# A graph network's first layernorm in blocks of sixteen tiles, one written order for VectorE and ScalarE, and signs taken of integers

## The chip, the core and the metric

The kernel runs on one core of a Trainium2 chip. The core has TensorE (PE in the profile; its weight loads are PEld), VectorE (DVE), ScalarE (ACT), GpSimd (POOL) and SyncE (SP, which only issues DMAs here). Each engine works through its own queue in order; semaphores tie the queues together. The metric is the device time of one execution in microseconds (us); three runs of the kernel before gave a median of 927.64 us.

## What is computed

Two layers of a graph network over N = 6250 nodes of 64 features and E = 206250 edges, sorted by destination:

```python
edge_index = jnp.stack([src, dst])
h = jnp.maximum(_layernorm(x, axis=-1), 0.0)
x = x + _L0_gnn_ref(h, edge_index, ...)      # twice: agg = segment_sum(h[src], dst); relu((h+agg) @ Wa + ba) @ Wb + bb
h = jnp.maximum(_layernorm(x, axis=-1), 0.0)
x = x + _L1_gnn_ref(h, edge_index, ...)      # segment_sum of an MLP of h[src], then an MLP of [h, sum]
```

`_layernorm` is (x - mean) / sqrt(var + 1e-5) over the 64 features. The three segment sums run over the same edges.

## The kernel before

**The graph as a matrix.** The nodes are cut into NT = 49 tiles of 128. The kernel counts, for each tile of destinations, how often each source occurs, and so builds the adjacency matrix A, 49 tiles of 128 x 6272 bytes. A segment sum is then a product of A with the node values on TensorE. The first sum uses each tile of A while it is in SBUF; all tiles are also written to DRAM, and the second and third sums (the two calls of `sweep`, whose products are on L733) read A back from there.

**Building a tile of A** (`build`, L423 to 439). Edges are handled in batches: batch 0 is one pair of tiles, batches 1 to 12 are two pairs (four tiles) each. For a batch b:

- `search(b)` (L291): ScalarE takes signs of 375 samples of `dst` against a bound (L303), VectorE makes the row and base from the sums (L307, L308).
- `fetch_blocks(b)` (L310): GpSimd issues an indirect DMA per pair that fetches a block of 550 integers of `dst` (L316). There are four buffers for them (`blk`, bufs=4).
- `search_block(b, i)` (L320): ScalarE casts the block in place from int32 to float32 (L326), then takes the Sign of it with a sum (L328).
- `fetch_edges(b)` (L331): VectorE makes offsets (L336, L337), GpSimd issues one indirect DMA per pair for destinations (`d_win`) and one for sources (`s_win`), both on L341.
- `slots(b)` (L347): VectorE splits the edges' numbers into word, byte and high part (L366 to L382); `cast` (L384) and `turn` (L390) bring them into the layout of `lkw` through ScalarE and TensorE.
- `hot` (L402), part of `build`: VectorE makes one-hot tables `there`, `high` and `low` (L409, L413, L416). TensorE multiplies them (`cnt`, L432, 64 products of 49 columns a tile, in four quarters of 16), ScalarE writes the counts out as `a` (L434), SP sends the tile to DRAM (L438). Tile 0 is counted in three pieces of 16, 16 and 32 columns (`FIRST_HOTS`), each with tables of its own.

**The first sum.** While tile t is counted, `FirstSum.quarter` multiplies tile t-1 with the layernormed node values `hp` (L587: 49 products of 193 columns; L589: the node itself), a quarter after each quarter of counts. It needs `hp` of all 49 tiles: quarter i uses its i-th fourth. For each four tiles a small MLP (`first_halves` to `third_product`) follows, placed by the table `beside` at quarters of later tiles.

**The first layernorm** (`values(t)`, L503) fills `hp`, eight tiles (XT) a call: TensorE transposes x (L509), a copy goes to SBUF (L512: VectorE for the first four calls, ScalarE for the last three), TensorE subtracts the mean by a product with `center` (L518) into a PSUM bank, `scaled` (L239) squares on ScalarE (L243), sums on VectorE (L245), takes the root on ScalarE (L246), the reciprocal and the scaled, clipped value on VectorE (L247, L248); `split` (L251) makes three bfloat16 parts, whose sum is the value, by turns on ScalarE (L254, L257) and VectorE (L256, L258). The last call has one tile. The calls stand between the steps of batches 0 to 3: `values(0)` after `fetch_blocks(1)`, two more before `slots(0)`, one after `turn(0, 0)`, three after `build(0)`.

**What sets the order.** A scheduler places the instructions; a written order binds it only where the kernel says so. `behind(op, other)` puts `op` after `other` on the same engine without a semaphore. `follow(op, engine)` does that with the engine's last step of `build` (`counted`), so it has no effect until the first `hot`. `search` and `slots` also have a parameter `after`. GpSimd has only the indirect DMAs to issue, in the order written.

Of the kernel before, what the change touches and what calls it, by code (L numbers as in the profile page):

```python
# [31 lines left out]
FP = mybir.dt.float32  # L32
# [6 lines left out]
AF = mybir.ActivationFunctionType  # L39
OP = mybir.AluOpType  # L40
# [5 lines left out]
D = 64  # L46
# [106 lines left out]
def fast(ctx: ExitStack, tc: tile.TileContext, x, src, dst, w, bad, out):  # L153
# [13 lines left out]
    def bank(name, dtype=FP):  # L167
        return pmix.tile([P, CH * 4 // mybir.dt.size(dtype)], dtype, tag="mix", name=name)
# [43 lines left out]
    ps = bank("ps_smp")  # L212
    nc.tensor.matmul(ps[:, :NB], ones[:SP_ROWS, :], smp_d.rearrange("p a b -> p (a b)"), start=True, stop=True)
    smp = once.tile([P, NB], FP, name="smp")
    nc.scalar.copy(smp, ps[:, :NB])


    HP = NP * D + 1
# [29 lines left out]
        return nc.vector.scalar_tensor_tensor(to, xm, 0.0, var[:, :, None].to_broadcast([P, n, D]), op0=OP.max,  # L248
                                              op1=OP.mult)

    def split(parts, v, n, f):  # L251

        p1, p2, p3 = (parts[:, :, i * f:(i + 1) * f] for i in range(NP))
        nc.scalar.copy(p1, v)  # L254
        r = work.tile([P, CH // f, f], FP, name="r", tag=f"r{f}")[:, :n, :]
        nc.vector.tensor_tensor(r, v, p1, op=OP.subtract)  # L256
        nc.scalar.copy(p2, r)  # L257
        nc.vector.tensor_tensor(p3, r, p2, op=OP.subtract)  # L258

    def halves(parts, v):  # L260

        first = nc.scalar.copy(parts[:, :, 0, :], v)
# [16 lines left out]
    def tiles_of(b):  # L279
        return range(starts[b], starts[b] + BATCHES[b]), slice(starts[b], starts[b] + BATCHES[b])  # L280

    counted = {}

    def behind(op, other):

# [4 lines left out]

    def follow(op, engine):  # L291

        if engine in counted:
            behind(op, counted[engine])

    def search(b, after=None):

        if b >= len(BATCHES):
            return
        each, qs = tiles_of(b)  # L300
        for q in each:
            junk = wins.tile([P, NB], BF, name="junk", bufs=1)
            op = nc.scalar.activation(junk, smp, AF.Sign, bias=below_node[:, q:q + 1], accum_out=sign1[:, q:q + 1])  # L303
            if after:
                behind(op, after)
            follow(op, "ACT")
        nc.vector.tensor_scalar(row[:, qs], sign1[:, qs], -0.5, NB / 2 - 1, op0=OP.mult, op1=OP.add)  # L307
        nc.vector.tensor_scalar(base[:, qs], sign1[:, qs], -0.5 * BLK, (NB / 2 - 1) * BLK + BLK / 2,  # L308
                                op0=OP.mult, op1=OP.add)

# [9 lines left out]
    def search_block(b, i):  # L320

        if b >= len(BATCHES):
            return
        q = starts[b] + i
        blk = blks.pop(q)
        follow(nc.scalar.copy(blk.bitcast(FP), blk), "ACT")  # L326
        junk2 = wins.tile([P, BLK], BF, name="junk2", bufs=1)
        return nc.scalar.activation(junk2, blk.bitcast(FP), AF.Sign, bias=below_node[:, q:q + 1],  # L328
                                    accum_out=sign2[:, q:q + 1])

    def fetch_edges(b):  # L331

        if b >= len(BATCHES):
            return
        each, qs = tiles_of(b)
        nc.vector.scalar_tensor_tensor(off_f[:, qs], sign2[:, qs], -0.5, base[:, qs], op0=OP.mult, op1=OP.add)  # L336
        nc.vector.tensor_scalar(off[:, qs], off_f[:, qs], float(E - P), None, op0=OP.min)  # L337
        lists[b] = [wins.tile([P, MOST, P], I32, name=name)[:, :len(each), :] for name in ("d_win", "s_win")]
        for win, of in zip(lists[b], (dst, src)):
            for i, q in enumerate(each):  # L340
                nc.gpsimd.indirect_dma_start(  # L341
                    out=win[:, i, :], out_offset=None, in_=of.rearrange("(a o) -> a o", o=1),
                    in_offset=bass.IndirectOffsetOnAxis(ap=off[:, q:q + 1], axis=0))

    numbers = {}

    def slots(b, after=None):  # L347

        if b >= len(BATCHES):
            return  # L350
# [8 lines left out]

        def first(op):  # L360
            follow(op, "DVE")
            if after:
                behind(op, after)

        pair = temp("pair")
        first(nc.vector.tensor_scalar(pair, d, 1, PITCH // 2 - 1, op0=OP.logical_shift_right, op1=OP.bitwise_and))  # L366
# [25 lines left out]
    def turn(b, i):  # L392

        if b >= len(BATCHES):
            return
        ps = bank("ps_win", BF)
        for k in range(3):
            follow(nc.tensor.transpose(ps[:, k * P:(k + 1) * P], parts2[b % 2][:, i, k, :], identb), "PE")
        lkw = lkws[starts[b] + i] = wins.tile([P, 3, P], BF, name="lkw", bufs=5)
        return nc.scalar.copy(lkw.rearrange("p a b -> p (a b)"), ps[:, :3 * P])  # L400

    def hot(lkw, g0, n):  # L402

# [96 lines left out]
            nc.tensor.matmul(ps[:, j * HID:(j + 1) * HID], t2[:, j * P:(j + 1) * P], w.w3, start=True, stop=True)  # L500
        halves(h2r[:, t:t + n], ps[:, :n * HID].rearrange("p (t f) -> p t f", f=HID))

    def values(t):  # L503

        n = min(XT, NT - t)
        ps = bank("xt")
        sides = [(j, min(2, n - j) * D) for j in range(0, n, 2)]
        for j, f in sides:
            nc.tensor.transpose(ps[:f, j * D:j * D + P], xs[:, t + j:t + j + f // D, :].rearrange("p t d -> p (t d)"), w.ident)  # L509
        f = sides[-1][1]  # L510
        xt = work.tile([P, CH], FP, name="xt", tag="t1")
        op = (nc.vector.tensor_copy if t < 4 * XT else nc.scalar.copy)(xt[:f, :len(sides) * P], ps[:f, :len(sides) * P])  # L512
        if t < 2 * XT:
            behind(op, sampled)
            behind(op, bounds)
        xm = pacc.tile([P, CH], FP, name="acc")
        for j, f in sides:
            nc.tensor.matmul(xm[:, j * D:j * D + f], xt[:f, j * D:j * D + P], center[:f, :f], start=True, stop=True)  # L518
        h = work.tile([P, XT, D], FP, name="h")[:, :n]
        op = scaled(h, xm[:, :n * D].rearrange("p (t d) -> p t d", d=D), n)  # L520
        split(hp[:, t:t + n], h, n, D)
        return op


    beside = {}
# [22 lines left out]
                beside.setdefault(4 * (4 * g + u) + 1, []).append((what, (of,)))  # L548

    nc.gpsimd.memset(hp[:, :, NP * D:], 1.0)  # L550
    search(0)
    fetch_blocks(0)
    search(1)
    fetch_blocks(1)
    values(0)
    search_block(0, 0)
    fetch_edges(0)
    values(XT)
    op = values(2 * XT)
    slots(0, op)  # L560
    cast(0, 0)
    cast(0, 2)
    for i in range(2):
        search_block(1, i)
    fetch_edges(1)
    op = turn(0, 0)
    values(3 * XT)
    search(2, op)
    fetch_blocks(2)
    search(3, op)  # L570
    fetch_blocks(3)

    r1, acc1 = {}, {}

# [32 lines left out]
    for t in range(NT + 1):  # L607
        last_total, total = total, FirstSum(t - 1, a) if t else None
        if t < NT:
            def between(i):  # L610
                if total:
                    total.quarter(i)
                if last_total and i == 2:
                    last_total.check()
                for what, args in beside.get(4 * t + i, ()):
                    what(*args)

            a = build(t, between)
            if t == 0:
                values(4 * XT)  # L620
                for i in range(2):
                    search_block(2, i)
                fetch_edges(2)
                values(5 * XT)
                values(6 * XT)
            if t == 1:
                w1p = weight_halves(w.w1x, "w1p", once)
                m1p, u1p = weight_halves(w.m1x, "m1p"), weight_halves(w.u1x, "u1p")
        else:
            last_total.check()  # L630
            for i in range(4):
                total.quarter(i)
            total.check()
# [368 lines left out]
```

## Time and profile before

| what | value |
|---|---|
| three runs | 929.69, 927.28, 927.64 us; median 927.64 |
| the profiled execution | 924.73 us, of which the span of its core is 922.9 us |
| busy in the span | PE 867.1 us (94%), DVE 619.3 us (67%), ACT 573.9 us (62%), POOL 114.7 us (12%) |
| first `there` on DVE (tile 0) | 25.02 us |
| first product with `hp` (L587) | 53.75 us |
| last product with `hp` (L589), end of the first sum | 394.68 us |
| first and second sweep (L733) | 396 us to the end |
| the casts of L326 | 25, 644 ns each |

How to read it: times in lines of the timeline are the start in us from the span's beginning, then the duration in us, the engine, the line of the kernel, the operation, output and input with their shapes, and in brackets how long the engine was idle before and who released it. A row of a window gives, after the window, its length, and for each engine its busy time and the number of instructions that begin there, then the TensorE clock that was granted (1.00 is full), the share of the DMA engines and GB/s. The profiled execution took 2.9 us less than the median of the runs; durations come from it, and a change is carried as a difference.

### The profile page before, as it was taken

The numbers are of one execution on the slowest core, as the hardware profiler recorded it, in microseconds if no ns is written. First come the engines' busy times: TensorE is split into PE (matmuls) and PEld (weight loads), VectorE is DVE, ScalarE is ACT, GpSimd is POOL, SyncE is SP. The second block draws the span as 40 slices with busy tenths as digits, with TensorE's granted clock in tenths as the row PEclk, the third lists the DMA queues.
The fourth block names the chain that finished last, engine by engine and source line by source line (L and its number), as shares of the span: only waits on it lengthen the run. The fifth ranks groups of instructions, "written<-read, shape, count | busy, mean of one in ns | idle before, by whom it ended". The sixth has DMA issues, their size and how long they took to land.

```text
span 922.9 us, 19818 instructions
## 1 busy us (share of the span) xinstructions
PE 867.1 (94%) x8323; PEld 743.4 (81%) x8323; DVE 619.3 (67%) x914; ACT 573.9 (62%) x772; POOL 114.7 (12%) x86
## 2 busy tenths in 40 slices
PE   3579999999999999999999999999999999999996
PEld 2479898898988999988787777778889767777785
DVE  5899988898888989644554445545445756666652
ACT  5577786667866666654445454454545677877763
POOL 3356423244232200000000000000000000000000
PEclk8599999999999999999999999999999999999999
DMA  6233433334333332555544444444433768888872
GB/s 145 98 118 143 176 133 129 131 143 172 137 118 142 119 141 107 182 134 141 140 118 121 123 115 117 128 119 128 118 103 94 193 176 231 233 224 221 234 188 64
DMA packets 195655, 133.71 MB, mean 145 GB/s; under 512 B 35204, under 2 KB 186884, under 8 KB 195556
## 3 DMA queue, kind: packets, MB, share of 16 engines
q1 hardware_dynamic: 188728, 121.22, 44.5%
q0 software_dynamic: 3600, 10.32, 3.7%
q8 instruction: 67, 1.10, 0.5%
q10 hardware_dynamic: 3228, 0.81, 0.4%
q14 instruction: 32, 0.26, 0.1%
HBM read 91.38 MB, written 40.94 MB: 143 GB/s over the span
## 4 chain that ended last, share of the span: by engine, by line
PE 83%; ACT 6%; issue 5%; DMA 3%; POOL 1%; DVE 1%; DVEq 0%; ACTq 0%; POOLq 0%
PE acc L733 42%; PE acc L587 20%; PE cnt L432 8%; PE ps_t L461 7%; PE ps_y L470 4%; ACT a L434 2%; DMA a<-A 2%; ACT ar L726 1%; PE ps_g L500 1%; PE tf L445 1%; DVE ar L726 1%; POOL d_win L341 1%; ACT blk L326 1%; POOL blk L316 1%; DMA s_win<-in_src_dram,off 1%
## 5 line engine op out<-in xcount | busy, mean ns | idle before, releaser
L726 DVE CAST ar<-a 128x2048 fp32r<-128x2048 uint8 (+2 forms) x208 | 220.4, 1071 | 202.8 <-PE acc L733 163.7
L726 ACT CAST ar<-a 128x2048 fp32r<-128x2048 uint8 (+2 forms) x130 | 234.3, 1804 | 139.3 <-PE acc L733 104.4
L733 PE MATMUL acc<-ar,h2r 128*128 128x512 f32 (+2 forms) x1274 | 297.4, 388 | 0.0
L733 PEld LDWEIGHTS acc<-ar,h2r 128*128 128x128 f32 x1274 | 229.7, 188 | 50.0 <-issue 5.7
L587 PE MATMUL acc<-hp,a 128*128 128x193 bf16 x2401 | 237.0, 247 | 10.7 <-ACT a L434 4.0
L434 ACT ACTIVATE a<-cnt 128x784 int16<-128x784 f32 x196 | 159.6, 820 | 87.1 <-PE cnt L432 63.8
L587 PEld LDWEIGHTS <-a 128*128 128x128 fp8e4 x2401 | 195.9, 98 | 14.3 <-ACT a L434 6.8
L733 PE MATMUL acc<-ar,yr 128*128 128x512 f32 (+2 forms) x637 | 158.4, 399 | 0.5 <-DVE yr L263 0.5
L733 PEld LDWEIGHTS acc<-ar,yr 128*128 128x128 f32 x637 | 115.5, 188 | 33.1 <-issue 10.3
L432 PE MATMUL cnt<-high,low 128*128 128x49 bf16 x3136 | 117.8, 187 | 14.7 <-DVE low L416 9.0
L432 PEld LDWEIGHTS <-low 128*128 128x128 fp8e4 x3136 | 109.6, 97 | 23.2 <-issue 13.3
L416 DVE TENSOR_TENSOR low<-there,lkw 128x2048 int32<-128x2048 bf16 (+2 forms) x51 | 112.0, 2196 | 0.0
L413 DVE TENSOR_TENSOR high<-high,lkw 128x3136 bf16<-128x3136 bf16 (+2 forms) x51 | 87.8, 1722 | 31.0 <-PE cnt L432 30.4
L316 POOL DMA_INDIRECT blk<-in_dst_dram,row x25 | 54.2, 2167 | 126.3 <-DVE base L308 110.4
L409 DVE TENSOR_TENSOR there<-word,lkw 128x2048 bf16<-128x2048 bf16 (+2 forms) x51 | 58.9, 1173 | 0.0
L341 POOL DMA_INDIRECT d_win<-in_dst_dram,off x25 | 26.3, 1052 | 68.8 <-DVE high_i L373 54.3
L341 POOL DMA_INDIRECT s_win<-in_src_dram,off x25 | 32.0, 1281 | 7.6 <-issue 7.6
L463 ACT ACTIVATE t<-ps_t,d 128x512 f32<-128x512 f32 (+2 forms) x26 | 17.3, 666 | 11.7 <-PE ps_t L461 11.7
L463 ACT ACTIVATE t<-ps_t,c 128x512 f32<-128x512 f32 (+1 forms) x26 | 17.1, 663 | 7.5 <-PE ps_t L461 7.5
L463 ACT ACTIVATE t<-ps_t,e 128x512 f32<-128x512 f32 (+2 forms) x26 | 17.2, 663 | 5.4 <-PE ps_t L461 5.4
L448 ACT ACTIVATE h3f<-tf 128x512 fp32r<-128x512 f32 (+2 forms) x13 | 7.5, 574 | 19.2 <-PE tf L445 19.2
L328 ACT ACTIVATE junk<-blk,below_node 128x550 bf16<-128x550 f32 x25 | 18.8, 753 | 0.6
(135 smaller groups left out, 620.1 us busy)
## 6 DMA issues: line engine op xcount, KB each, us to landing
a<-A SPq DMA_DIRECT2D x264, 256.0 KB
A<-a SPq DMA_DIRECT2D x49, 784.0 KB
a<-A SPq DMA_DIRECT2D x24, 192.0 KB
a<-A SPq DMA_DIRECT2D x24, 128.0 KB
a<-A SPq DMA_DIRECT2D x22, 64.0 KB
out_dram<-o SPq DMA_DIRECT2D x11, 128.0 KB
xs<-in_x_dram ACTq DMA_DIRECT2D x3, 256.0 KB
xs<-in_x_dram SPq DMA_DIRECT2D x3, 256.0 KB
```

The source lines that it names most:

```text
L316: nc.gpsimd.indirect_dma_start(out=blks[q], out_offset=None, in_=dst.rearrange("(r b) -> r b", b=BLK), in_offset=bass.IndirectOffsetOnAxis ...
L341: nc.gpsimd.indirect_dma_start(out=win[:, i, :], out_offset=None, in_=of.rearrange("(a o) -> a o", o=1), in_offset=bass.IndirectOffsetOnAx ...
L409: nc.vector.tensor_tensor(there, word2[:, None, :, :].to_broadcast(shape), of(0)[:, :, None, :].to_broadcast(shape), op=OP.is_equal)
L413: nc.vector.tensor_tensor(high, high2[:, None, :, :].to_broadcast(shape), of(1)[:, :, None, :].to_broadcast(shape), op=OP.is_equal)
L416: counted["DVE"] = nc.vector.tensor_tensor(low.rearrange("p (g i) w -> p g i w", i=2), there.rearrange("p g w i -> p g i w"), of(2)[:, :, ...
L432: counted["PE"] = nc.tensor.matmul(ps[:, b, j * H:(j + 1) * H], low[:, g, :], high[:, g // 2, :, g % 2], start=True, stop=True)
L434: counted["ACT"] = nc.scalar.activation(a[:, :, k:k + 2 * PG].rearrange("p h (b j) -> p h b j", b=2), ps[:, :, :PG * H].rearrange("p b (j ...
L461: nc.tensor.matmul(ps[:, :n * P], wt, rhs, start=(i == 0), stop=(i == len(terms) - 1))
L463: nc.scalar.activation(to, ps[:, :n * P], AF.Relu, bias=bias)
L587: nc.tensor.matmul(acc[:, t % 2, :], self.a[:, k, :], hp[:, k], start=(k == 0), stop=False)
L726: widen(ar.rearrange(f"p k t b -> {order}"), a.rearrange(f"p t (k b) -> {order}", b=P))
L733: nc.tensor.matmul(acc[:, :n * P], part, ar[:, k - k0].rearrange("p t b -> p (t b)"), start=(k == 0 and i == 0), stop=(k == H - 1 and i == ...
```

## The change

- `values` is replaced by a class `Values` with one method a step. Blocks a, b and c have 16 tiles each, d has the 49th. Transposes and copies still go eight tiles at a time (`center`), and all copies are on VectorE now; square, sum, root, scaled value, three parts and two remainders are single instructions over 1024 elements instead of two over 512. The centered values lie in a pair of PSUM banks of the counts' pool (`cnt`), the temporaries in the buffers of `there`, `low` and `high`.
- Until tile 0 is counted, `follow` ties every step of VectorE and ScalarE that it is called for to the step before it on that engine (`starting`), so that their order is the written one. The list at the start is written anew: blocks a, b and c come almost whole before `slots(0)`; the last part of c and most of d come after `build(0)`.
- `search_block` loses its cast: Sign reads the int32 block directly. This holds for all 25 blocks.

GpSimd's order of DMAs is the same in both.

```diff
     def follow(op, engine):
 
-        if engine in counted:
+        if starting is not None:
+            if engine in starting:
+                behind(op, starting[engine])
+            starting[engine] = op
+        elif engine in counted:
             behind(op, counted[engine])
...
-        follow(nc.scalar.copy(blk.bitcast(FP), blk), "ACT")
         junk2 = wins.tile([P, BLK], BF, name="junk2", bufs=1)
-        return nc.scalar.activation(junk2, blk.bitcast(FP), AF.Sign, bias=below_node[:, q:q + 1],
-                                    accum_out=sign2[:, q:q + 1])
+        op = nc.scalar.activation(junk2, blk, AF.Sign, bias=below_node[:, q:q + 1], accum_out=sign2[:, q:q + 1])
+        follow(op, "ACT")
...
-    def values(t):
...
+    class Values:
...
+        def center(self, c):
...
+            follow(nc.vector.tensor_copy(xt[:f, :len(sides) * P], ps[:f, :len(sides) * P]), "DVE")
+            if c == 0:
+                self.xm = (pacc.tile([P, CH], FP, name="acc") if n == 1 else
+                           pcnt.tile([P, 2, CH], FP, name="cnt").rearrange("p b c -> p (b c)"))
...
+        def square(self):
...
+            follow(nc.scalar.activation(self.sq, self.xm, AF.Square), "ACT")
+        def variance(self):
...
+            follow(nc.vector.tensor_reduce(self.var, self.sq, axis=AX.X, op=OP.add), "DVE")
...
+        def third(self):
+            follow(nc.vector.tensor_tensor(self.part(2), self.r, self.part(1), op=OP.subtract), "DVE")
...
     search(0)
     fetch_blocks(0)
+    a.center(0)
+    a.center(1)
     search(1)
     fetch_blocks(1)
-    values(0)
+    b.center(0)
+    a.square()
+    b.center(1)
+    a.variance()
+    a.root()
     search_block(0, 0)
+    b.square()
+    a.scale()
     fetch_edges(0)
-    values(XT)
-    op = values(2 * XT)
-    slots(0, op)
+    c.center(0)
+    b.variance()
+    a.first()
+    c.center(1)
+    b.root()
+    a.rest()
+    b.scale()
+    a.second()
+    c.square()
+    c.variance()
+    b.first()
+    a.third()
+    c.root()
+    b.rest()
+    search_block(1, 0)
+    c.scale()
+    b.second()
+    search_block(1, 1)
+    fetch_edges(1)
+    c.first()
+    b.third()
+    slots(0)
     cast(0, 0)
     cast(0, 2)
-    for i in range(2):
-        search_block(1, i)
-    fetch_edges(1)
-    op = turn(0, 0)
-    values(3 * XT)
-    search(2, op)
+    c.rest()
+    turn(0, 0)
+    c.second()
+    d.center(0)
+    search(2)
     fetch_blocks(2)
-    search(3, op)
+    d.square()
+    d.variance()
+    d.root()
+    d.scale()
+    d.first()
+    search(3)
     fetch_blocks(3)
+    starting = None
...
             if t == 0:
-                values(4 * XT)
+                c.third()
+                d.rest()
+                d.second()
+                d.third()
                 for i in range(2):
                     search_block(2, i)
                 fetch_edges(2)
-                values(5 * XT)
-                values(6 * XT)
```

## The prediction

> **What bounds the kernel now.** I read the page first: PE is busy 94% of the span, and 83% of the chain that ended last is PE's. Then the busy time by stage, since the change only touches the start:
>
> ```profile
> core 0: us, PE busy (x) PEld busy (x) DVE busy (x) ACT busy (x) POOL busy (x), PEclk, DMA share, GB/s
> ...
> 20.00:40.00 20.00, 6.80 (x82) 5.85 (x83) 17.45 (x48) 10.77 (x26) 8.41 (x8) 0.50 0.28 80
> 40.00:60.00 20.00, 14.32 (x164) 12.81 (x163) 17.37 (x38) 17.57 (x42) 10.41 (x8) 0.79 0.35 126
> 60.00:80.00 20.00, 19.55 (x361) 19.25 (x359) 20.00 (x22) 13.58 (x25) 8.71 (x4) 1.00 0.24 94
> 80.00:395.00 315.00, 302.56 (x5263) 290.19 (x5261) 273.33 (x355) 218.62 (x372) 80.08 (x52) 1.00 0.39 144
> ```
>
> PE is short of work until about 60 us and nearly full from there to the end. DVE is the other full engine: 20.00 of 20 us between 60 and 80. So the time after 60 us is fixed work, and the question is when, and with how much done, the kernel gets into it. The chain of waits shows what ends the start: GpSimd's DMAs for blocks and edges from 46 to 57.6 us, then DVE's slots, then PE. The timeline of GpSimd has the links:
>
> ```profile
> 46.03 2.24 POOL L316 DMA_INDIRECT blk<-in_dst_dram,row  x1 [11.34 <-ACT junk L328]
> 48.58 2.03 POOL L316 DMA_INDIRECT blk<-in_dst_dram,row  x1 [0.30 <-issue]
> 50.91 0.94 POOL L341 DMA_INDIRECT d_win<-in_dst_dram,off  x1 [0.30 <-DVE off L337]
> 52.16 1.44 POOL L341 DMA_INDIRECT d_win<-in_dst_dram,off  x1 [0.30 <-issue]
> 53.91 0.94 POOL L341 DMA_INDIRECT s_win<-in_src_dram,off  x1 [0.30 <-issue]
> 55.16 0.94 POOL L341 DMA_INDIRECT s_win<-in_src_dram,off  x1 [0.30 <-issue]
> ```
>
> Two blocks of batch 4 stand ahead of the edges of batch 2, in both kernels. They take 10.07 us, and the edges land 1.5 us after the last. DVE stands with tile 3's tables behind those edges:
>
> ```profile
> 45.67 1.78 DVE L413 TENSOR_TENSOR high<-high,lkw 128x3136 bf16<-128x3136 bf16 x1
> ...
> 47.51 2.28 DVE L416 TENSOR_TENSOR low<-there,lkw 128x2048 int32<-128x2048 bf16 x1
> ...
> 57.72 0.29 DVE L373 TENSOR_SCALAR high_i<-s_win 128x256 int32<-128x256 int32 x1 [0.16 <-DMA s_win<-in_src_dram,off]
> ...
> 60.47 1.78 DVE L413 TENSOR_TENSOR high<-high,lkw 128x3136 bf16<-128x3136 bf16 x1
> ...
> 62.37 2.28 DVE L416 TENSOR_TENSOR low<-there,lkw 128x2048 int32<-128x2048 bf16 x1
> ```
>
> I take the start of tile 3's `low`, 62.37 us, as the mark: before it waits rule, after it DVE and PE run without holes. The change is worth what it does to this mark, to PE's arrears at it, and to the steady stage.
>
> **The change, part by part.**
>
> *Prices.* DVE steps of 512 float32 follow each other at 0.60 us (17.10, 17.70, 18.30); 1024 elements took 1.14 (`low` of 128x1024 at 36.42, next at 37.56). ACT: 0.51 for 512; from 0.60 long at 512 and 0.82 at 784, 1.01 long and 0.91 apart at 1024. So a pair of 512 steps becomes one step cheaper by 0.06 us on DVE (four steps, three blocks: 0.7 us) and 0.1 us on ACT. The size itself saves under 2 us, all in a stretch with holes. The order is what counts. I walked the built program's order with these prices.
>
> *To the first edges.* The row for batch 0 now precedes the first copy: blocks leave 0.25 us earlier. But block a needs two copies (9.34 and 9.94), its mean product runs 10.05 to 12.7 (2.68 us before), b's eight transposes to 13.8, b's copies to 14.5, and a's 1024-sum stands behind these in the written order: 14.5 to 15.6, root 0.30, scaled value 16.2 to 17.3. Batch 0's offsets stand behind it and a copy of c (0.60): ready at 18.1 instead of 15.7. Behind this wait is only GpSimd: `d_win` leaves at 18.2, not 15.98; that is hidden, since slots(0) is later still.
>
> *To slots(0).* Between the offset and slots(0) DVE now has eight 1024 steps (9.1), a copy (0.6) and small ones (0.6), and waits twice for ACT: for the second part of a and the square of c in a row (0.7), and for the sign of block (1, 1) (0.7). 18.1 + 11.7 = 29.8 us. Before, slots(0) began at 20.41. The edges have lain there since about 23.
>
> *To the first count.* slots(0) holds now one remainder (1.14) instead of two 512 steps, and ends in the same 1.2 us of cast, transpose and copy as before: 4.1 us instead of 4.6. First `there` 33.9 (25.02 before), first `low` 34.7 (25.84). PE has nothing to do for these 9 us; that costs nothing by itself, since this layernorm work is then no longer in the way.
>
> *To tile 1.* From the first `low` to the end of tile 1's took 16.8 us before (25.84 to 42.6). Four 512 steps leave it (2.4), one 1024 step and the 49th tile's small ones enter (1.7), the waits stay about equal: 16.1. It ends at 50.8 instead of 42.6. The row of batch 4's search is the next step of DVE, as before.
>
> *To the mark.* Before, GpSimd had to wait at this point for a block buffer until 46.03; now the buffers are free, and it starts at 51.0, 5.0 us later. Are its six DMAs again 10.07 us? Alone such an issue takes 0.94 and 0.30 between: 7.5 for six. The row says why they took more: the one from 46.03 ended at 48.27, 0.90 after DVE's `high` left (47.37); the next at 50.61, 0.90 after `low` left. They now start again beside `there`, `high` and `low`, of tile 2. The Trainium skill (SBUF — State Buffer, section Who interferes with whom) speaks against this change here: GpSimd and VectorE share one pair of ports, VectorE takes it with two SBUF inputs or in a two-port mode, and the second to come is blocked until the first is through. By that rule and the row: 10.1; without it 7.5, and the mark 2.6 us earlier. I take 10.1: edges issued at 61.1, landed at 62.6. From there DVE has high part, word, parts, `high` and two shifts ahead of `low`: 0.20 + 0.20 + 0.33 + 1.70 + 0.40 = 2.8 (4.65 before, with layernorm and weight steps between, which now come earlier). The mark: 65.4, that is 3.0 us later.
>
> *PE's arrears.* Layernorm being done, tiles 0 and 1 get their first-sum products sooner: at the mark about 22 products of 193 columns more are done, at 0.085 us each 1.9 us. If PE alone ruled afterwards, 3.0 - 1.9 = 1.1 us would remain. But PE then stands idle for 4 to 5 us ahead of tile 3, and this trace grants half clock after such holes (0.50 from 18 to about 44 us; again 0.53 between 50 and 52 after a hole of 2 us), for some 4 to 5 us of busy time (39.75 to 44.6), in which a quarter of counts takes 0.84 instead of 0.42. That costs 1.7 to 2.5 us. And DVE, without a hole until 80 us before, can't make up anything. Bounds 1.1 and 3.0; I take 2.9, by the window row in which DVE is 20.00 of 20.
>
> *The casts.* 25 casts at 0.55 apart leave ACT, 13.8 us, nearly all beside PE. What PE waits for ACT in that stage:
>
> ```profile
> PE cnt L432 <- issue: 5.5, 14, 0.5
> PE acc L587 <- ACT a L434: 4.0, 8, 1.1
> PE acc L587 <- issue: 1.9, 5, 1.1
> ```
>
> Gain between 0 and 4.0 us. In the one that I followed (PE at 111.84) ACT had been idle for 1.60 us before its copy at 110.96, so no cast was in its way; nor is an issue hole a cast. I take 0. A Sign of int32 has no row; the cast of 550 int32 took 0.64 us and casts of 512 float32 0.61 to 0.62 (17.48, 20.00), so integers are read at the same pace, and I take the Sign at its old 0.75; bounds 0 and 0.1 us each, hidden in the steady stage.
>
> *The rest.* The last three copies move from ACT to DVE (in the walk). GpSimd and SP keep their order; the sweeps only shift.
>
> Sum: 924.73 + 2.9 = 927.6 for the profiled execution; with the median 927.64 + 2.9 = 930.5 us.
>
> **The rivals.**
>
> *A: the written order pays (faster).* DVE's waits between 9 and 62 us sum to 9.6 us. If GpSimd's issues slip between DVE's steps (7.5 us) the mark is 62.8, +0.4; with PE's 1.9 us of arrears gone and its clock warm, -1.5; with half to all of the 4.0 us of ACT waits, -3.5 to -5.5: about 924. It decides once the casts give back more than 1.3 us on top of the -1.5. For it: PE's wait for `a` comes once per four tiles, near block searches. Against: ACT idle before it. Chance 0.18.
>
> *B: the two cancel (same).* The mark at +3.0, PE warm or half of the arrears kept, and 0.5 to 1 us from the casts: +1 to +2, about 929. For it: the bounds above. Chance 0.32.
>
> *C: one more lost port (slower still).* One block DMA of batch 5 took 6.78 us (73.74 to 80.52) beside four DVE steps without a hole. If a batch 4 block meets this, the edges come 3 us later and the mark at 68: 933 to 934. Within the slower case, about 0.12 of it.
>
> *D: the order doesn't bind*, DVE running as it did: excluded by the built order.
>
> **How the numbers follow.** Likeliest: the mark at +3 with cold PE and no gain from casts, 930.5, with C chance 0.50; its own range 929.5 to 934. A has 0.18, B 0.32. What a measurement of this kernel can tell from no change is 0.3%, 2.8 us: below 924.9 is faster, above 930.4 slower. Range for 8 in 10: 925.5 (the inner half of A) to 934 (C's end).
>
> **What would show it.** In the new profile: first `there` near 34 us (29.8 for slots(0)); the row of batch 4 near 51; six GpSimd issues of about 10 us beside tile 2's tables; tile 3's `low` near 65.4; PE idle for 4 us or more before it, with clock 0.50 after; the gap to before shrinking little up to the end of the first sum, near 397.5 instead of 394.68. I am wrong if the mark comes before 63, if PE stays warm, or if the wait for `a` once per four tiles goes away with the casts.

## The result and the profile after

The changed kernel takes 934.07 us (median of 8 runs, 930.86 to 937.94) against 927.7 us for the kernel before beside it (8 runs, 925.85 to 930.04): a ratio of 1.0068, 95% interval 1.0045 to 1.0092. It is slower, as forecast, but by 6.4 us where 2.9 were predicted, and the median lies just above the range's end of 934.0. The profiled execution took 933.89 us with a span of 932.1, which is 9.2 more than in the profiled execution of before; that one, at 924.73 us, was a quick one of its kind.

The busy time by stage, in the stretches shown of before:

```profile
core 0: us, PE busy (x) PEld busy (x) DVE busy (x) ACT busy (x) POOL busy (x), PEclk, DMA share, GB/s
20.00:40.00 20.00, 4.08 (x35) 2.92 (x34) 16.10 (x39) 11.32 (x22) 6.43 (x7) 0.63 0.11 28
40.00:60.00 20.00, 11.92 (x184) 10.48 (x184) 17.58 (x29) 12.62 (x30) 17.20 (x9) 0.69 0.38 129
60.00:80.00 20.00, 15.14 (x219) 13.85 (x220) 14.54 (x27) 9.12 (x20) 6.54 (x7) 0.83 0.29 105
80.00:395.00 315.00, 301.70 (x5280) 289.35 (x5279) 276.66 (x352) 207.60 (x357) 93.13 (x52) 0.99 0.37 138
```

PE and DVE, both full from 60 us on in before, now have holes (stretches in which an engine stands idle) until 80 us, with 15.14 and 14.54 us busy of 20, and the mean clock there is 0.83. GpSimd is busy for 17.20 us of the third stretch instead of 10.41. Its timeline says with what:

```profile
43.14 7.34 POOL L309 DMA_INDIRECT blk<-in_dst_dram,row  x1 [0.67 <-DVE row L300]
50.79 2.23 POOL L309 DMA_INDIRECT blk<-in_dst_dram,row  x1 [0.30 <-issue]
53.32 1.05 POOL L309 DMA_INDIRECT blk<-in_dst_dram,row  x1 [0.30 <-issue]
...
61.14 0.99 POOL L336 DMA_INDIRECT s_win<-in_src_dram,off  x1 [0.30 <-issue]
62.43 0.94 POOL L336 DMA_INDIRECT d_win<-in_dst_dram,off  x1 [0.30 <-issue]
```

A block gather (an indirect DMA that fetches a block) of batch 3 met the tables of tiles 0 and 1, and ended only at 50.48, after DVE's `high`. The six DMAs ahead of tile 3 started at 53.32 and not at 51.0; the row for the first of them was ready a microsecond earlier:

```profile
47.87 1.79 DVE L408 TENSOR_TENSOR high<-high,lkw 128x3136 bf16<-128x3136 bf16 x1
...
52.12 0.17 DVE L300 TENSOR_SCALAR row<-sign 128x2 int32<-128x2 f32 x1
```

DVE waited for what comes from the DMAs:

```profile
59.55 0.16 DVE L329 SCALAR_TENSOR_TENSOR off_f<-sign,base 128x2 f32<-128x2 f32 x1 [2.03 <-ACT junk L320]
61.02 0.29 DVE L359 TENSOR_SCALAR pair<-d_win 128x256 int32<-128x256 int32 x1 [1.30 <-DMA d_win<-in_dst_dram,off]
64.54 0.29 DVE L366 TENSOR_SCALAR high_i<-s_win 128x256 int32<-128x256 int32 x1 [0.85 <-DMA s_win<-in_src_dram,off]
67.41 2.28 DVE L411 TENSOR_TENSOR low<-there,lkw 128x2048 int32<-128x2048 bf16 x1
73.50 0.36 DVE L668 TENSOR_REDUCE r<-acc 128x64 f32<-128x192 f32 x1 [3.60 <-PE acc L662]
```

The mark, tile 3's `low`, is at 67.41 instead of 62.37. Then something comes that no step of the prediction has: DVE waits 3.60 us for PE (the last line), with tile 4's tables queued behind the reduction. PE was late because one quarter of tile 2's counts, usually 16 matmuls in 0.58 us, took six microseconds:

```profile
63.65 0.18 PE L427 MATMUL cnt<-high,low 128*128 128x49 bf16 x1 [0.41 <-issue]
64.37 0.21 PE L427 MATMUL cnt<-high,low 128*128 128x49 bf16 x2 [0.53 <-issue]
65.79 0.22 PE L427 MATMUL cnt<-high,low 128*128 128x49 bf16 x2 [1.20 <-issue]
67.22 0.28 PE L427 MATMUL cnt<-high,low 128*128 128x49 bf16 x3 [1.21 <-issue]
...
68.84 2.12 PE L660 MATMUL acc<-hp,a 128*128 128x193 bf16 x12
```

The word after the arrow is "issue": PE waited for nothing that the trace shows. The six such holes sum to 4.3 us. The last row is a step of 12 products that takes 1.2 us at full clock: half clock was granted from 66.2 us for 6.8 us. Tile 4's `low` is 8.9 us later than before, tile 13's 5.5, tile 48's 8.6.

### The profile page after: what moved, and what is told of

The parts are those of the page before. It is cut to its first block, busy times and chain, and to the rows that moved or that the text cites. A ratio compares the mean times of both kernels' runs of the same rounds, so it can differ in the third digit from the quotient of the medians.

```text
span 932.1 us, 19776 instructions
## 1 busy us (share of the span) xinstructions
PE 868.1 (93%) x8323; PEld 743.1 (80%) x8323; DVE 619.6 (66%) x902; ACT 556.8 (60%) x732; POOL 128.9 (14%) x86
## 4 chain that ended last, share of the span: by engine, by line
PE 86%; ACT 4%; DMA 3%; DVE 3%; issue 2%; POOL 0%; SPq 0%; ACTq 0%; DVEq 0%
PE acc L807 41%; PE acc L660 21%; PE cnt L427 10%; PE ps_t L456 6%; PE ps_y L465 3%; DMA a<-A 3%; ACT ar L800 2%; ACT a L429 1%; PE tf L440 1%; PE ps_g L495 1%; DVE ar L800 1%; DMA smp_i<-in_dst_dram 1%; PE ps_win L391 0%; ACT t L458 0%; DVE var L535 0%
## 5 line engine op out<-in xcount | busy, mean ns | idle before, releaser
L660 PE MATMUL acc<-hp,a 128*128 128x193 bf16 x2401 | 242.4, 250 | 8.5 <-ACT a L429 5.8
L660 PEld LDWEIGHTS <-a 128*128 128x128 fp8e4 x2401 | 199.3, 99 | 12.7 <-ACT a L429 7.3
L309 POOL DMA_INDIRECT blk<-in_dst_dram,row x25 | 66.4, 2657 | 118.5 <-DVE base L301 98.7
L336 POOL DMA_INDIRECT s_win<-in_src_dram,off x25 | 33.9, 1357 | 7.6 <-issue 7.6
L668 DVE TENSOR_REDUCE r<-acc 128x64 f32<-128x192 f32 x49 | 15.2, 350 | 10.1 <-PE acc L662 10.1
L458 ACT ACTIVATE t<-ps_t,c 128x512 f32<-128x512 f32 (+1 forms) x26 | 17.1, 663 | 7.1 <-PE ps_t L456 7.1
```

The source lines that it names most:

```text
L309: nc.gpsimd.indirect_dma_start(out=blks[q], out_offset=None, in_=dst.rearrange("(r b) -> r b", b=BLK), in_offset=bass.IndirectOffsetOnAxis ...
L336: nc.gpsimd.indirect_dma_start(out=win[:, i, :], out_offset=None, in_=of.rearrange("(a o) -> a o", o=1), in_offset=bass.IndirectOffsetOnAx ...
L458: nc.scalar.activation(to, ps[:, :n * P], AF.Relu, bias=bias)
L660: nc.tensor.matmul(acc[:, t % 2, :], self.a[:, k, :], hp[:, k], start=(k == 0), stop=False)
```

## The experiments

Four theories were put to the test. **One**: the mark sets the end, and the change moves it, by the order of the start. **Two**: the missing casts shift ScalarE and GpSimd against PE in the steady stage and make its holes larger. **Three**, formed from the trace above: PE's "issue" holes belong to the edge gathers on GpSimd. **Four**, formed late: whether there are such holes depends on the chip. The runs that follow came in five sets, each on another chip (the expectations say "call"). All times below are told as ratios to before, measured in the same set. "Mark" is the start of tile 3's `low` in one profiled execution; "idle" is DVE's idle time ahead of it, the mark less DVE's busy time up to it. "Casts out" means that the cast of `search_block` is left out; "place" is explained at e10.

| kernel | ratio (95%) | mark, us | idle, us |
|---|---|---|---|
| before: first trace, e8, e16 | 1 | 62.37, 62.31, 61.48 | 14.2, 14.3, 13.3 |
| changed: first trace, e12, e17 | 1.0068, 1.0070 (1.0047 to 1.0092), 1.0118 (1.0090 to 1.0146) | 67.41, 67.03, 66.47 | 19.3, 19.0, 18.3 |
| e1 before, no casts | 1.0087 (1.0060 to 1.0114) | 64.92 | 17.2 |
| e2 changed, casts back | 1.0084 (1.0060 to 1.0108) | 65.45 | 17.7 |
| e3 changed, untied | 1.0061 (1.0039 to 1.0084) | 66.96 | 19.1 |
| e4 changed, edges first | 1.0127 (1.0102 to 1.0152) | 67.33 | 19.1 |
| e5 before, late casts out | 1.0006 (0.9989 to 1.0023) | 63.88 | 15.8 |
| e6 changed, late edges 3 | 1.0103 (1.0066 to 1.0140) | 66.69 | 18.8 |
| e7 changed, early search | 1.0069 (1.0045 to 1.0092) | 65.87 | 17.2 |
| e9 changed, 8 wide | 1.0061 (1.0038 to 1.0084) | 66.07 | 17.1 |
| e10 before, place 17 | 0.9803 (0.9769 to 0.9836) | 63.28 | 15.2 |
| e11 before, place 21 | 0.9803 (0.9768 to 0.9837) | 66.04 | 18.0 |
| e13 changed, place 17 | 1.0051 (1.0032 to 1.0071) | 65.42 | 17.5 |
| e14 e13, later edges 3 | 1.0081 (1.0065 to 1.0096) | 68.02 | 20.1 |
| e15 e5 at place 17 | 0.9988 (0.9978 to 0.9997) | 62.51 | 14.2 |
| e18 before, place 17 | 0.9809 (0.9782 to 0.9836) | 62.46 | 14.4 |

**First set: order or casts.** e1 takes out the cast of `search_block` in the kernel before:

```diff
-        follow(nc.scalar.copy(blk.bitcast(FP), blk), "ACT")
-        return nc.scalar.activation(junk2, blk.bitcast(FP), AF.Sign, ...)
+        op = nc.scalar.activation(junk2, blk, AF.Sign, ...)
+        follow(op, "ACT")
```

> The kernel before, with only its 25 casts taken out (Sign reads the int32 block). Theory 1, the loss lies in the order of the start: 927.7 us within 1 us, and tile 3's low near 62.4 as before. Theory 2, the missing casts shift ACT and GpSimd against PE in the steady stage, so that its holes grow: about 931 us, and the starts of low come later than before's by more and more between 130 and 395 us, by some 3 us at the end.

> The changed kernel with its 25 casts put back. Theory 1: 934 us within 1 us. Theory 2: about 931 us, with low's lag behind before staying at 5.5 to 6 us from 130 us to the end, instead of growing to 8.6.

e3 replaces `starting.update(...)` by `starting = None`:

> The changed kernel with the same 16-tile steps in the same places of the program, but without the tie between them: up to the first count VectorE and ScalarE run in the order that the scheduler finds. By a walk of its built order with before's durations tile 3's low comes 2.8 us earlier than in the changed kernel, near 64.5. Theory 1: 930 to 931.5 us. Theory 2: 934 us, since the casts are still out.

e4 adds `behind(op, edges[2])` to the block DMAs of batch 4, where `edges[b]` is the last gather of a batch:

> The changed kernel with batch 4's two blocks put behind batch 2's four edge gathers on GpSimd. The gathers then leave from 53.3 instead of 56.45 and land near 60 instead of 63.5; DVE runs the table there after them instead of before, which gives 1.3 us of it back, so tile 3's low near 65.6 instead of 67.41. Theory 1: 932 us, within 1. A theory that the mark doesn't set the end (rival of both): 934 us.

No expectation of theory 1 or 2 for e1 held in full. Taking 25 casts out of before costs as much as the whole change. Part of the loss is there at the mark (+2.6): with the casts gone, the scheduler gives the start another order, in which DVE stands 3 us longer. Whether more is added later, e1's trace does not settle, since no trace of before is from its set: the lag of its `low` at tile 13 is 3.3 us against e8, but 5.3 and 5.9 us against the two other traces of before. e2 is no better than the changed kernel, e3 not clearly better; in e3's trace the mark is where the changed kernel has it, with the same idle time, so the tie alone is not the cause. e4 only shifted the wait: with the edges first, DVE's tables of tile 3 were placed behind them, it waited 2.26 and 2.18 us, and PE's "issue" holes were there again, 1.08 to 1.10 us each.

**Second set: the late casts, and the gathers of batch 3.** e5 casts only where `q < starts[4]`, so the order of the start stays before's own. e6 asks for batch 3's edges later, and e7 writes another order of the start:

> The kernel before with only the 18 casts of batches 4 to 12 taken out; the seven of the start stay, so VectorE's order up to tile 9 is before's own. Taking out all 25 had cost 0.87%. If that loss came in through the order of the start (theory 1), this one is within 0.2% of before, tile 3's low stays near 62.4, and the casts of the steady stage are worth nothing in either direction. If it came from the steady stage (theory 2), 0.6 to 0.9% slower again. If casts beside PE do cost, up to 0.3% faster.

```diff
-        at(13, fetch_edges, b + 3)
+        if b:
+            at(13, fetch_edges, b + 3)
+        else:
+            beside.setdefault(12, []).append((fetch_edges, (3,)))
```

> The changed kernel with the offsets and edge gathers of batch 3 put behind tile 3's low on VectorE, so that its four gathers leave near 70 us instead of 62.43. Theory 3: the six holes that PE has for no reason shown between 63.2 and 68.7 us (4.3 us) belong to those gathers; then PE runs through to tile 3's counts, tile 4's low lags before by about 5 us instead of 8.9, and the whole is 2 to 4 us faster than the changed kernel, 0.2 to 0.4% slower than before. If the holes belong to something else, they stay, and the time stays 0.7% above before's.

> The changed kernel with another written order: the searches of batches 2 and 3 and the block signs and edges of batch 2 come ahead of the first count, so that nothing of batch 2 has to be fetched while tiles 1 and 2 are built, and no block gather meets their tables. First low near 38 instead of 36.2. By a walk of its built order VectorE then stands for nothing between the first low and tile 3's, which comes at 62.4 plus up to 1 us, 4 to 5 us sooner than in the changed kernel. Theory 1 (the mark, set by VectorE's idle time ahead of it, sets the end): 928 to 930 us on the scale in which before is 927.7, that is within 0.3% of before. If the mark doesn't set the end: 0.7% above before as the changed kernel.

> The kernel before, unchanged, for a second trace: which places differ from run to run of one program, without any edit. Expected: tile 3's low within 0.5 us of 62.4, the single block gather of 6.8 us at 73.7 again, and PE's holes for no shown reason again in pairs beside the later edge gathers, once per four tiles.

e5 speaks against theory 2: its ratio is 1.0006, and its interval leaves at most 0.23%. It has the changed kernel's steady stage (but for one more tie, of `row` in each search) with before's start, so most of the change's loss comes in with the start. Its own mark, some 1.5 us late, cost nothing that can be measured. e6 shows that the six holes belong to the gathers: with these moved to 71.6 us, PE runs through the same stretch, and only a wait with a shown reason is left (PE's timeline of e6):

```profile
64.08 1.19 PE L663 MATMUL acc<-hp,a 128*128 128x193 bf16 x12
65.10 0.58 PE L427 MATMUL cnt<-high,low 128*128 128x49 bf16 x16
...
69.04 0.59 PE L427 MATMUL cnt<-high,low 128*128 128x49 bf16 x16 [1.65 <-DVE low L411]
```

Tile 4's `low` is 4.7 us behind before, as expected, not 8.9. But the kernel became slower: the moved gathers took 4.45 and 7.70 us among tables, and tile 7 stood 5 us for the edges. So it was shown to what the holes belong, not that removing them pays. e7 missed: GpSimd's chain was out of the way, and the mark came only 1.5 us earlier, with no gain in time. Its idle time was already 13.4 us at the first `low` (before 9.9, changed 13.6), and then `high` waited 2.06 us, for what the trace does not name. The chain of gathers is thus not the whole of the late mark: of the 5.0 us that DVE stands longer in the changed kernel, 3.7 arise ahead of the first `low`. e8 repeated the mark (62.31), and the block gather took 5.08 us. It also showed what varies without any edit: from tile 8 to 11 it fell 1.9 us behind the first trace of before, among other things by a wait of 1.23 us for ScalarE at 85.5.

**Third set: the size of the steps, and the place of the gathers.** e9 cuts every 16-tile step in two of 8 with the same buffers. The place in `at` is the quarter at which a step is asked for, counted from the start of a period of four tiles; e10 and e11 edit it in the kernel before (17 or 21, from batch 4 on; this is e10's edit):

```diff
-        at(13, fetch_edges, b + 3)
+        at(17 if b else 13, fetch_edges, b + 3)
```

> The changed kernel with the same buffers and the same written order, but every layernorm step of 16 tiles cut in two of 8 behind each other. What the size of the steps did, with the tie kept. VectorE's own work until tile 3's low has been 48.0 to 48.2 us in both kernels, so the prediction's 0.06 us for each pair were not seen; by a walk of the built order, two short steps wait less for ScalarE than one long: tile 3's low 1.8 us earlier than the changed kernel's. If the size is part of the loss: ratio to before near 1.005. If only the order counts: 1.007 as the changed kernel.

> The kernel before with the edge gathers of batches 4 to 12 asked for four quarters later in each period of four tiles (place 17 instead of 13), so that they leave beside the tables there, high and low of the next tile and not beside the slots. Start unchanged. Theory 3 (PE's holes for no shown reason belong to gathers that run unhindered one after the other; in the changed kernel, between 80 and 140 us, gathers that met the tables and took 1.4 to 2.1 us each went with only 0.7 us of PE idle, against 2.2 us in before): some of the 1.3 to 2 us of holes per period go, 0.3 to 1.5% faster than before. If the holes belong to the slots, to the copies of a, or to the store of A: no change within 0.2%.

> As the one with place 17, at place 21, another four quarters later, beside the next tile's tables, and with the store of A of another tile near it. Theory 3: as there, 0.3 to 1.5% faster; if the holes wander with the gathers to the new place, no change, but holes at the new place in the trace; if they stay at the old place without the gathers, the gathers have nothing to do with them.

> The changed kernel, unchanged, for a second trace and a second ratio. Expected: ratio 1.005 to 1.009; VectorE's idle time ahead of tile 3's low near 18.5 us against 14 in before, its work 48; the batch 3 block gather of 7.3 us near 43 again; holes in PE beside batch 3's edge gathers, with half clock after them, again.

With steps of 8, DVE's work to the mark is 49.0 us, with 16 48.1: the wide steps do save 0.9 us. But DVE then waits 2 us more for ScalarE and PE. The mark moves by 1.0 us against e12, and the ratios, 1.0061 and 1.0070, can't be told apart. e12 repeats every feature of the first trace, the 7.34 us block gather included, with seven holes instead of six.

e10 and e11 are the find of the study: 2.0% faster than before, more than the 0.3 to 1.5% expected. In the steady stage before has the holes that the changed kernel has at 63 us, once per four tiles, beside its edge gathers. What PE waited for between 80 and 395 us in before and at place 17 (e16, then e18, of one set):

```profile
PE cnt L432 <- issue: 5.8, 14, 0.5
PE acc L587 <- issue: 3.2, 6, 1.2
PE acc L587 <- ACT a L434: 3.2, 7, 0.5
```

```profile
PE acc L587 <- ACT a L434: 2.7, 7, 0.6
PE cnt L432 <- issue: 0.4, 1, 0.4
```

And the gathers beside which this was, again e16 and e18:

```profile
165.92 1.07 POOL L341 DMA_INDIRECT d_win<-in_dst_dram,off  x1 [4.39 <-DVE high_i L373]
...
169.90 1.60 POOL L341 DMA_INDIRECT s_win<-in_src_dram,off  x1 [0.30 <-issue]
```

```profile
140.05 6.12 POOL L341 DMA_INDIRECT d_win<-in_dst_dram,off  x1 [7.38 <-DVE off L337]
...
151.51 0.94 POOL L341 DMA_INDIRECT s_win<-in_src_dram,off  x1 [0.30 <-issue]
```

At place 13 four gathers leave within 5.6 us, beside the slots; at place 17 they meet the tables, are spread over 12.4 us, and 8.6 us of PE's "issue" holes go. That is not the whole gain: from the `low` of tile 13 to that of tile 48, e18 is 14.8 us shorter than e16; PE's idle time there falls from 11.6 to 1.9 us, and its busy time by 5.1 us. The matmuls' ends are modelled, so some of a hole can count as busy; how much of the 5.1 us that is was not tested. e11 also ran an experiment by itself: its start has e10's own order of steps, but DVE happened to stand 2.8 us longer. All its later `low` are 2.7 us behind e10's. That is theory 1 with no edit at all: here a late mark was not made good.

**Fourth and fifth set: the change without the steady holes.** e13 is the changed kernel at place 17, e14 also asks for the gathers of batch 3 in the second quarter of tile 2, e15 is e5 at place 17; e16 to e18 set before, changed and place 17 side by side. The edits of e13 and e18 name place 17 for batch 3 too, unlike e10's; in their traces each engine's steps still come in the order of the changed kernel and of before up to 80 us.

> The changed kernel with the edge gathers of batches 4 to 12 asked for at place 17, as it made the kernel before 2.0% faster. Batch 3's keep their place in the start, and so should PE's holes beside them. Up to here the changed kernel won some of its late start back between 80 and 120 us, where before had its first steady holes and it had none; with place 17 neither has them. If the start's loss and the steady holes are two separate things: the holes beside batch 3's gathers stay, and the lag behind before at place 17 is that of the second reduction, about 7 us: ratio to before near 0.988. If the change's loss is partly in the steady stage: less than that, 0.981 to 0.984.

> As the one before it, with batch 3's edge gathers put between the tables of tile 3 as well, so that they meet there, high and low; by a walk of the built order they leave at 63.5, 66.1, 68.7 and 70.9 us instead of 61.2 to 66.0. Theory 3: PE's six holes after 63 us and the half clock that follows them go, and what is left of the change is VectorE's idle time ahead of tile 3's low, 3 to 5 us against before at place 17: ratio to before near 0.985. If the holes stay, or if they are not what makes the lag grow after that low: the same time as the kernel before it in this list.

> The kernel before with place 17 and with the casts of batches 4 to 12 taken out; its start is before's own. With PE's holes gone, a copy of ScalarE's that comes late could now be the next limit: PE still waited 2.0 us in six places for the copy of a. If the casts were in its way, up to 0.2% faster than the same without this edit, ratio 0.978; if not, 0.980.

> The kernel before, unchanged, for a trace beside the next two on one chip. In the last call it took 906 us, in the earlier ones 923 to 929, and the kernels at place 17 showed no holes of PE without a shown reason there, not even beside batch 3's gathers, where the changed kernel had always had them. Theory 4: such holes belong to the chip (or the load of the program) and need gathers beside them; on a chip without them before is near 906 and its trace has none, on one with them near 923 to 929 with 10 us of them between 60 and 395 us.

> The changed kernel, unchanged, on the same chip. Theory 4: on a chip with holes, 0.7% above before and six or seven holes after 63 us as twice before; on a chip without, none of them, and what is left is VectorE's idle time ahead of tile 3's low, 3 to 4 us, 0.3 to 0.45% above before. A rival, that the change's loss is the same everywhere: 0.7% on both kinds.

> The kernel before with all edge gathers at place 17, again. Theory 4: on a chip with holes 2% faster than before, as measured once; on a chip without, the same as before within 0.2%. If the 2% were the luck of one load: no gain on a chip with holes.

In the fourth set the kernel before took 906.32 us (17 runs) where it takes 923 to 929 in all others, and place 17 won nothing there (e15: 0.9988). That speaks for theory 4, or for anything else that differed in that set. Its traces have no "issue" hole from 55 us to the end of the first sum, but this proves less than the expectation of e16 says: in e13 the gathers of batch 3 left between 60.87 and 68.52 us and met more of the tables (1.46, 1.04, 1.93 and 2.31 us each, where the changed kernel had three of 0.94 and one of 1.73), so theory 3 allows for their absence too. Before has no trace from that set, and the fifth fell on a chip with holes, so the expectation for a chip without them wasn't tried. What the fourth set does show: without one such hole the change's start still costs. Against e15, e13's `low` lag is 2.9 us at the mark and 4.5 at the end, e14's 5.5 and 8.2, and the ratios are 0.63% and 0.93% above e15's. (In both, the first gathers at place 17 add a DVE wait near 115 us, of 2.5 and 2.9 us.) There were no holes for e14 to remove.

In the fifth set place 17 gave 0.9809: the gain is real where the holes are. The pair e16 and e17 shows the change on one chip (DVE is the third busy time; before, then changed, from 0 to the mark):

```profile
0.00:61.48 61.48, 30.45 (x314) 26.30 (x315) 48.23 (x127) 39.83 (x92) 27.19 (x34) 0.75 0.44 121
```

```profile
0.00:66.47 66.47, 32.23 (x332) 27.18 (x332) 48.16 (x114) 33.63 (x70) 35.15 (x34) 0.72 0.41 112
```

DVE's work is the same, 48.2 us; its idle time is 13.3 and 18.3. The lag of `low` is then 5.0 us at tile 3, 8.3 at tile 4 (five "issue" holes, 2.4 us, and half clock from 57.6 to 64.4 and from 67.9 to 71.3), 4.7 at tile 13, when before has paid its first steady holes and the changed kernel almost none (PE busy between 110 and 140 us: 27.97 against 29.60), and 6.6 from tile 40 to the end of the first sum. The span is 8.4 us longer; the last 1.8 us arise in the sweeps, which the change does not touch.

The step at tile 40 is one window of half clock in the steady stage. Every trace of the changed kernel has one (at 236.9, 324.8, 323.9 us), no trace of before; it costs 1.7 us. It need not come from the start: e5, with before's start and only the late casts out, has one too (323.5 us), and from tile 13 to 48 it takes 254.2 us like the changed kernel, where before takes 251.1 to 252.4. e2, the changed kernel with its casts back, has none (251.1 us); nor have e1 and e3, though without casts. So up to 1.7 us may belong to the casts after all, within the interval of e5. In the first trace:

```profile
230.00:236.90 6.90, 5.38 (x97) 4.83 (x95) 6.90 (x18) 1.98 (x4) 4.53 (x4) 1.00 0.44 159
236.90:240.30 3.40, 3.07 (x24) 2.94 (x25) 2.99 (x3) 1.54 (x2) 0.00 (x0) 0.50 0.24 82
240.30:245.00 4.70, 4.70 (x87) 4.69 (x87) 2.45 (x3) 2.91 (x5) 0.00 (x0) 1.00 0.04 15
```

The Trainium skill (TensorE: Matmul & The Clock Gate, section "What's actually happening") has the clock fall after an idle window of about 3.4 us. The length agrees: half clock comes in pieces of 3.4 us and multiples. The condition does not, if idle means without any product: in the 3.4 us ahead of this one PE had holes of 0.83, 0.17 and 0.40 us and the start of another, 1.5 us in all (6.90 less 5.38 in the first row), and products between them.

## Why the prediction was right and wrong

The direction was right and the size was not: 6.4 us for 2.9. Two steps failed, the mark by 2 us and, above all, what comes after it.

- *Start to tile 1, steps two to five*: right within 1.5 us. slots(0) began at 30.9 (29.8 predicted), the first `low` at 36.2 (34.7), the row of batch 4 at 52.1 (50.8). The samples landed 0.8 us later than in before, but that is not the whole of it: in e12 they landed as early as in before, and slots(0) came at 30.6.
- *"The size itself saves under 2 us"*: right, 0.9 us of work (e9). What the step left out: with wide steps DVE waits 2 us more.
- *The mark, "now the buffers are free, and it starts at 51.0"*: this is the first step that failed. The six DMAs began at 53.32, 2.3 us late. 1.3 of it was there in the row for batch 4; the other 1.0 is the block gathers of batch 3, taken as over by then. The first met the tables and took 7.34 us. The six then took 8.8 us, not 10.07, which gives 1.3 back; the edges came 2.4 us after the last of them and not 1.5 (2.4 to 2.5 in e12 and e17 too). Mark: +5.0 measured, +3.0 predicted. The port rule of the Trainium skill (SBUF — State Buffer, section Who interferes with whom) was weighed for the six DMAs only, and not for the four blocks ahead of them, which the change had moved beside tables. This trace agrees that the later one is blocked: the gather ended 0.82 us after the end of `high` (49.66), as in before (48.27 after 47.45). The page limits the rule for two SBUF inputs to a GpSimd instruction that reads SBUF, and says that in a probe a tensor_tensor did not stall DMAs; here the gather's issue did wait for it. Rival C had the mechanism, on another block.
- *"After it DVE and PE run without holes"*: this is the step that failed most, since it put at nothing what came to 3.9 us. From 63 to 69 us PE lost 4.3 us in "issue" holes beside batch 3's gathers (e6 shows that they belong to these), 6.8 us from 66.2 on ran at half clock, and DVE stood 3.60 us for both: the lag of `low` grew from 5.0 us at tile 3 to 8.9 at tile 4. 3.4 us of that came back up to tile 13: between tiles 4 and 8 DVE had 1.1 us less to do than in before, and between 8 and 13 it stood 3.0 us less for PE's counts, while PE, which has its first steady holes there in before, lost 1.1 us less.
- *PE's arrears (what it is behind with at the mark), "about 22 products more are done"*: failed with it. 75 products of the first sum are in the trace ahead of the mark, against 68 in before: 7 more. In e6, without the holes, they were 101. And PE's wait for tile 3's `low`, put at 4 to 5 us, is 1.65 us there.
- *DVE can't make up a late mark*: right in e11, e13 and e14.
- *The casts, gain 0*: right for the steady stage within e5's interval, and the Sign of 550 int32 took 0.74 to 0.75 us. Not foreseen: taking them out reorders the start when the scheduler decides it (e1).
- *End of the first sum near 397.5*: 403.5. Of the 6 us more, 2.0 are there at the mark and a window of half clock makes 1.7; the other 2.3, what the holes left among them, were not separated.
- *Rival A* needed the wait for `a` to go away with the casts; it stayed (4.5 us between 80 and 395 us). *Rival B* is excluded by the interval.
- Two sums of the prediction are off, without weight in the result: six lone issues take 7.1 us, not 7.5 (five gaps, not six), and DVE's waits from 9 to 62 us are 7.1 us; 9.6 counts the one that ends at 8.82.

Still open: what PE waits for in the "issue" holes. Shown is only that they go when the edge gathers leave the place. Within a group of holes PE starts again at intervals of 0.71 to 0.77 us, or two or three times that, in all traces that have such groups (63.65, 64.37, 65.79, 67.22 in the lines above); what has this period is not known. Nor does every row of unhindered gathers bring them: batch 3's in before, 0.96 to 1.40 us each, came with one hole of 0.27 us. Open too is why the fourth set has none. The marks in the table don't rank the ratios either: e5's is 1.5 us late at no cost, and e1, 2.6 us late, lost as much as the changed kernel, 5.0 us late. So how much of the 6.4 us the mark, the holes and the half clock each hold stays open; in the traces on one chip they are 5.0, at most 3.3 with most of it given back, and 1.7.

## What to carry to other kernels

The first full step of the limiting engine comes after its work plus its idle time up to there: sum both for the new order, and look at every gather that the change moves for the steps that it now lies beside, not only at those on the path. A removed instruction is an edit of the order wherever a scheduler decides it; test it with the order held fixed. And look in the steady stage for holes that nothing explains and that come once per period: asking for the transfers beside them four quarters later was worth 2%, three times what the change cost, where those holes exist.

## What the runs showed of the hardware

- A GpSimd gather beside back-to-back VectorE steps with two SBUF inputs can stand for several of them in a row: it took 6.78, 7.34, 7.70 and 8.49 us where it takes 0.94 alone. Three of these ended 0.89 to 0.91 us after VectorE went on to a reduction out of PSUM (before at 79.63, changed at 87.42, e6 at 83.16), the fourth after a gap between two steps.
- In the steady stage of before, four unhindered gathers of 0.95 to 1.60 us in 5.6 us came with 0.4 to 1.7 us of "issue" holes on PE each time; the same four hindered and spread over 12.4 us with none (e18, from 140 us on).
- Half clock was granted for 3.4 us after a stretch of 3.4 us with 1.5 us of holes and products between them.
- The same kernel before took 906.3, 923.1, 926.1 to 929.3 us in different sets of runs; only ratios within a set compare.
